# Local attention with V as the stationary operand in column tiles, and the first expert's gather placed inside the shared expert

## The chip, the cores and the metric

The kernel runs on one core of a Trainium2 chip. The metric is device time in microseconds (us), from launch to end; beside it stands the span of a profiled execution, from its first to its last instruction. PE is the matrix engine (TensorE), DVE the vector engine, ACT the scalar engine, POOL is GpSimd and SP the engine that issues most DMAs.

## The reference, cut to what matters

Three residual blocks on x (2 batches of 512 tokens, 512 wide), each on a layer-normalized x, all in float32: cross attention over 8192 context tokens per batch, local attention over a window of 7 tokens, and a mixture of 16 experts with a shared expert.

```python
# local attention, 16 heads of 32
q, k, v  = split_heads(x @ W_qkv.T + b_qkv)
k_lat    = k @ W_lat.T + b_lat          # per head, 32 x 32
v_lat    = v @ W_lat.T + b_lat
kw, vw   = k_lat[:, :, widx], v_lat[:, :, widx]    # 7 neighbours of each token, wrapping at the ends
attn     = softmax(einsum('bhsd,bhswd->bhsw', q, kw) / sqrt(32))
out      = einsum('bhsw,bhswd->bhsd', attn, vw) ; return out @ W_proj.T + b_proj

# experts: each takes the 128 tokens that score highest for it
topk_score, topk_ids = top_k(sigmoid(h @ gate_w.T).T, 128)
xin = h[topk_ids]
eo  = (silu(xin @ gw.T + gb) * (xin @ up_w.T + up_b)) @ down_w.T + down_b
out = zeros.at[topk_ids].add(eo * topk_score) + (silu(h @ sh_g.T) * (h @ sh_u.T)) @ sh_d.T
```

## The kernel before, in words

The stages follow each other: cross attention to about 2700 us of the profiled span, local attention to about 2915, the shared expert to 3089, the 16 experts to the end. They share one core, and PE's queue takes them in this order.

**Local attention** (lines 477 to 732). A group is one batch and four heads (128 channels); there are 8 groups. The 512 tokens of a group are cut into 5 blocks: four of 103 queries and one of 100. A block of `nq` queries meets `nk = nq + 6` keys, so its scores are a `nq` x `nk` matrix per head in which a band of 7 is kept (`band` adds -1e30 elsewhere). Per group, five `pieces` make the operands, each run beside one block of the group before: `project` of K (line 535), `latent_k` (line 562, then `extended`, which copies three wrapped columns to either end), `project` of Q, `project` of V, and `latent_v` (line 573), which makes V for each block with keys on partitions, 32 columns per head and a column of ones.

The loop over blocks (line 722) is pipelined by hand. Iteration k does, in this order:

- `softmaxed` of block k: four score matmuls, one per head, on 32 rows of the array each (`sw`, line 591); four DVE reduces that add the band and take the row maximum (line 599); the negated, scaled maximum (line 605); four ACT exps (line 607).
- one piece of the next group.
- `turned` of block k-1: four transposes of the exps on PE (`tpw`, line 618), one ACT copy to `pT`.
- `weighed` of block k-2: four matmuls with the turned exps stationary and V moving, 33 columns (`pow`, line 630). The column of ones gives the sum of the exps; DVE takes its reciprocal (line 635) and multiplies (line 637).
- `placed` of block k-3: a transpose back to channels on partitions (`tpo`, line 646), an ACT copy into `aT` (line 651), and after a batch's last block the output projection (`proj_residual`, line 106).
- what `beside` holds for this k: norms, inputs of the second batch, bias tables of the experts.

[...]

**Shared expert** (lines 773 to 806): for each batch 8 gate/up blocks (`pf`, line 780) and 4 output products of 8 matmuls each (`pso`, line 798). `select` is one of 16 rounds on DVE that find the 8 highest scores of each expert. After the stage the lists are turned by two small transposes (line 812) into `idx` and `scol`, whose columns address the gathers.

**Experts** (lines 875 to 893): `gather` reads 128 rows of the normalized tokens by an indirect DMA on POOL (line 822), `tokens` turns them on PE, `expert_in` streams weight tiles of 1 MB (`load_tile`, line 447, nine buffers in turn) and multiplies (line 839).

The framework that builds the instruction streams takes the code's order as priority, not as law: an instruction may be put ahead of an earlier one on its engine where it is ready. SP's timeline shows it: the first experts' weights are issued at 2874.7 us, long before the shared expert's outputs are stored.

Of the kernel before, what the change touches and what calls it, by code (L numbers as in the profile page):

```python
# [10 lines left out]
F32 = mybir.dt.float32  # L11
# [3 lines left out]
AF = mybir.ActivationFunctionType  # L15
ALU = mybir.AluOpType
# [27 lines left out]
def perceiver_kernel(  # L44
# [432 lines left out]
    with ExitStack() as es:  # L477
# [46 lines left out]
        def block(n):  # L524

            return n * BQ, min(BQ, S - n * BQ)
# [37 lines left out]

        def latent_v(i):

            vt = gp.tile([P, NBQ, 4, DK + 1], F32, name="vt")
            nc.gpsimd.memset(vt[:, :, :, DK : DK + 1], 1.0)
            for n in range(NBQ):
                q0, nq = block(n)  # L570
                nk = nq + W7 - 1
                pl = ps.tile([P, 4, DK], F32, tag="ps", name="plv")
                nc.tensor.matmul(
                    pl[0:nk].rearrange("p h d -> p (h d)"), lhsT=raw_t[i, 2][:, ds(q0, nk)],
                    rhs=wlat_bd, start=True, stop=True,
                )
                nc.vector.tensor_tensor(
                    vt[0:nk, n, :, 0:DK], pl[0:nk],
                    blat_b[0:nk].unsqueeze(1).to_broadcast([nk, 4, DK]), ALU.add,
                )  # L580
            v_t[i] = vt

        def softmaxed(i, n):

            q0, nq = block(n)
            nk = nq + W7 - 1
            ss = []
            for h in range(4):
                r = slice(h * DK, (h + 1) * DK)
                s = ps.tile([P, NK], F32, tag="ps", name="sw")  # L590
                nc.tensor.matmul(
                    s[0:nq, 0:nk], lhsT=q_t[i][r, ds(q0, nq)], rhs=k_t[i][r, ds(q0, nk)],
                    start=True, stop=True,
                )
                ss.append(s)
            sb = gp.tile([P, 4, NK], F32, name="sb")
            mx = gp.tile([P, 4], F32, name="mxw")
            for h in range(4):
                nc.vector.tensor_tensor_reduce(
                    out=sb[0:nq, h, 0:nk], in0=ss[h][0:nq, 0:nk], in1=band[0:nq, 0:nk],  # L600
                    scale=1.0, scalar=-3.0e38, op0=ALU.add, op1=ALU.max,
                    accum_out=mx[0:nq, h : h + 1],
                )
            nm = gp.tile([P, 4], F32, name="nm")
            nc.vector.tensor_scalar(nm[0:nq], mx[0:nq], -SCALE, None, ALU.mult)
            for h in range(4):
                nc.scalar.activation(
                    sb[0:nq, h, 0:nk], sb[0:nq, h, 0:nk], AF.Exp, bias=nm[0:nq, h : h + 1],
                    scale=SCALE,
                )  # L610
            p_t[i, n] = sb

        def turned(i, n):
# [9 lines left out]
            p_t[i, n] = t  # L623

        def weighed(i, n):
            q0, nq = block(n)
            nk = nq + W7 - 1
            po = ps.tile([P, 4, DK + 1], F32, tag="ps", name="pow")
            for h in range(4):
                nc.tensor.matmul(  # L630
                    po[0:nq, h, :], lhsT=p_t[i, n][0:nk, h, 0:nq], rhs=v_t[i][0:nk, n, h, :],
                    start=True, stop=True,
                )
            rl = gp.tile([P, 4, 1], F32, name="rlw")
            nc.vector.reciprocal(rl[0:nq], po[0:nq, :, DK : DK + 1])
            o = gp.tile([P, 4, DK], F32, name="ow")
            nc.vector.tensor_tensor(
                o[0:nq], po[0:nq, :, 0:DK], rl[0:nq].to_broadcast([nq, 4, DK]), ALU.mult
            )
            o_t[i, n] = o  # L640

        def placed(i, n):
            b, g = groups[i]
            q0, nq = block(n)
            tp = ps.tile([P, BQ], F32, tag="ps", name="tpo")
            nc.tensor.transpose(
                tp[:, 0:nq], o_t[i, n][0:nq].rearrange("p h d -> p (h d)"), ident[0:nq, 0:nq]
            )
            if g == 0 and n == 0:
                aT[b] = batch_tile("aT")  # L650
            nc.scalar.copy(aT[b][:, g, ds(q0, nq)], tp[:, 0:nq])
# [68 lines left out]
        for f in pieces:  # L720
            f(0)
        for k in range(len(items) + 3):
            if k < len(items):
                softmaxed(*items[k])
            i, n = divmod(k, NBQ)
            if i + 1 < len(groups):
                pieces[n](i + 1)
            for back, f in ((1, turned), (2, weighed), (3, placed)):
                if 0 <= k - back < len(items):
                    f(*items[k - back])  # L730
            for f in beside.get(k, ()):
                f()
# [23 lines left out]
    def select():  # L756
# [7 lines left out]
        if i < CAP // 8 - 1:  # L764
            nc.vector.match_replace(
                out=work[i % 2], in_to_replace=m8, in_values=cur, imm_value=-1.0
            )

    st = es1.enter_context(tc.tile_pool(name="s_tmp", bufs=2))
    sTp = es1.enter_context(tc.tile_pool(name="s_T", bufs=1))  # L770
    shd = [load_tile(sh_d[i]) for i in range(2)]
    norm(1, "f1")
    for b in range(B):
        sT = sTp.tile([P, SH // P, S], F32, tag="sT", name="sT")
        for f in range(SH // P):
            pair = []
            for wts in (shg, shu):
                pf = ps.tile([P, S], F32, tag="ps", name="pf")
                for c in range(DC):
                    nc.tensor.matmul(  # L780
                        pf, lhsT=wts[f // 4][:, c, ts(f % 4, P)], rhs=hT[b][:, c, :],
                        start=(c == 0), stop=(c == DC - 1),
                    )
                pair.append(pf)
            sg = st.tile([P, S], F32, name="sg")
            nc.scalar.activation(sg, pair[0], AF.Silu)
            nc.vector.tensor_tensor(sT[:, f, :], pair[1], sg, ALU.mult)
            if b == 0 and 1 <= f <= 4:
                forward_in(NT // B + f - 1, "f1")
            elif b == 0 and f == 5:  # L790
                gated(0)
                gated(1)
            elif b == 1 or f > 5:
                select()
        for j in range(4):
            po = ps.tile([P, D], F32, tag="ps", name="pso")
            for f in range(SH // P):
                nc.tensor.matmul(  # L798
                    po, lhsT=sT[:, f, ts(j, P)], rhs=shd[f // 4][:, f % 4, :],
                    start=(f == 0), stop=(f == SH // P - 1),  # L800
                )
            n = b * 4 + j
            nc.vector.tensor_tensor(x_sb[:, n, :], x_sb[:, n, :], po, ALU.add)
            nc.sync.dma_start(out=out[ts(n, P), :], in_=x_sb[:, n, :])
            select()
            select()

    top_f = sp.tile([E, CAP], F32, name="top_f")
    nc.vector.tensor_copy(top_f, top_i)
    for src, dst in ((top_f, idx), (top, scol)):  # L810
        pt = ps.tile([P, E], F32, tag="ps", name="pt")
        nc.tensor.transpose(pt, src, ident[0:E, 0:E])
        nc.vector.tensor_copy(dst, pt)
    es1.close()

    tmp = ctmp
    ep = ctx.enter_context(tc.tile_pool(name="e_tmp", bufs=2))

    def gather(e):

        xin = ep.tile([P, D], F32, name="xin")
        nc.gpsimd.indirect_dma_start(  # L822
            out=xin, out_offset=None, in_=h_dram,
            in_offset=bass.IndirectOffsetOnAxis(ap=idx[:, e : e + 1], axis=0),
        )
        return xin

    def expert_in(e, fq, xinT):

        pair = []  # L830
        for src, lo in ((gw, 0), (up, F)):
            wt = load_tile(src[e, fq])
            pf = ps.tile([P, 512], F32, tag="ps", name="pf")
            nc.tensor.matmul(
                pf, lhsT=pick[:, e, :], rhs=bias3[:, ds(lo + fq * 512, 512)],
                start=True, stop=False,
            )
            for c in range(DC):
                nc.tensor.matmul(  # L839
                    pf, lhsT=xinT[:, c, :], rhs=wt[:, c, :], start=False, stop=(c == DC - 1)  # L840
                )
            pair.append(pf)
# [22 lines left out]
            in_=y, in_offset=None, compute_op=ALU.add,  # L865
        )

    def tokens(xin):
        xinT = ep.tile([P, DC, CAP], F32, name="xinT")
        transposed(xinT, xin, ps)  # L870
        return xinT
# [69 lines left out]
```

## Time and profile before

| what | value |
|---|---|
| device time, median of 3 runs | 3846.05 us (3838.11 to 3847.68) |
| device time of the profiled execution | 3841.49 us |
| its span, first to last instruction | 3839.5 us |
| mean granted clock of PE | 0.993 |
| local attention, first latent V to the end of its last output projection | 2718.7 to 2915.1 us |
| shared expert, gate blocks and output products | 2915.1 to 3088.9 us |

In the profile's rows, `out<-in` names the tiles that an instruction writes and reads, then come partitions x elements. A matmul's form is given as rows * columns of the array that it occupies: `32*128` is a row tile, `128*32` a column tile. A float32 matmul appears as two records. A matmul's duration is latency; since matmuls overlap, what one takes from PE's time is the distance between the starts of neighbours. A row of a timeline begins with start and busy time in us and may end with the idle time before it and what released it.

### The profile page before, as it was taken

How to read it: one execution, taken by the hardware profiler on the slowest of the kernel's cores; microseconds unless marked ns; L12 is line 12 of the kernel's file. 1: busy time of each engine (PE TensorE's matmuls, PEld its weight loads, DVE VectorE, ACT ScalarE, POOL GpSimd, SP SyncE). 2: the span in 40 equal slices, each digit the busy share in tenths (PEclk: the TensorE clock that was granted, in tenths of full speed). 3: DMA queues.
4: the chain of work that ended last, by engine and by line, in shares of the span. 5: the costliest groups of instructions: out<-in, count | busy, mean ns of one | idle time of the engine just before them, and what ended most of it. 6: DMA issues, size and time to landing. Idle time of an engine off the chain costs nothing.

```text
span 3839.5 us, 99475 instructions
## 1 busy us (share of the span) xinstructions
PE 3773.4 (98%) x43100; PEld 1867.9 (49%) x43100; DVE 2284.6 (60%) x5444; ACT 1588.4 (41%) x2805; POOL 2069.1 (54%) x531
## 2 busy tenths in 40 slices
PE   8999999999999999999999999999999999999998
PEld 3345554554554554555555455444555444444444
DVE  6677777777777777777777777899743500000000
ACT  1125555555555555555555555676442001111110
POOL 0019998998998998999899899500100000000000
PEclk9999999999999999999999999999999999999999
DMA  5222212222223332222122222122201168888885
GB/s 188 87 73 71 69 60 70 71 71 71 71 68 103 125 125 92 70 71 71 57 71 71 71 71 70 60 86 63 75 31 36 58 229 286 285 287 287 288 285 172
DMA packets 143735, 438.07 MB, mean 114 GB/s; under 512 B 9408, under 2 KB 11728, under 8 KB 117856
## 3 DMA queue, kind: packets, MB, share of 16 engines
q1 hardware_dynamic: 137856, 419.33, 32.7%
q0 software_dynamic: 5200, 12.30, 1.3%
q8 instruction: 337, 5.52, 0.6%
q14 instruction: 102, 0.84, 0.1%
q10 hardware_dynamic: 240, 0.08, 0.0%
HBM read 423.21 MB, written 8.47 MB: 112 GB/s over the span
## 4 chain that ended last, share of the span: by engine, by line
PE 88%; DVE 2%; issue 1%; ACT 1%; DMA 0%; POOLq 0%; DVEq 0%; SPq 0%; ACTq 0%
PE av L353 13%; PE sx L295 12%; PE sc L331 12%; PE pv L255 11%; PE pf L839 11%; PE pk L239 10%; PE py L857 5%; PE pf L780 3%; PE sc L337 3%; PE pqkv L535 2%; PE po L106 1%; PE pso L798 1%; PE tp L98 1%; PE pow L630 1%; DVE junk L300 1%
## 5 line engine op out<-in xcount | busy, mean ns | idle before, releaser
L365 POOL TENSOR_TENSOR acc<-acc,pt 128x2048 f32<-128x2048 f32 x437 | 1991.2, 4557 | 452.0 <-ACT pt L344 451.2
L344 ACT ACTIVATE pt<-sc,mbias 128x512 f32<-128x512 f32 x2016 | 1218.3, 689 | 952.3 <-PE sc L337 950.9
L300 DVE CUSTOM_DVE_ANT_0 junk<-sx,mk 128x512 bf16<-128x512 f32 x1776 | 1228.1, 691 | 550.0 <-PE sx L295 352.7
L331 PE MATMUL sc<-qT,kt 32*128 32x512 f32 x4096 | 546.5, 594 | 0.0
L353 PE MATMUL av<-pt,vt 128*32 128x512 f32 x4032 | 540.6, 605 | 2.8 <-DVE mst L300 2.8
L255 PEld LDWEIGHTS pv<-wv_sb,ctx_t 128*32 128x32 f32 x16384 | 457.6, 110 | 155.0 <-DVE mst L300 101.4
L295 PE MATMUL sx<-kt,qT 32*128 32x512 f32 x3552 | 509.3, 640 | 0.9 <-DVE vt L260 0.9
L239 PE MATMUL pk<-ctx_t,wk_sb 128*32 128x256 f32 x8192 | 499.4, 385 | 2.1 <-DVE mst L300 2.1
L255 PE MATMUL pv<-wv_sb,ctx_t 128*32 128x128 f32 x16384 | 495.0, 273 | 1.3 <-DVE avs L361 1.3
L839 PE MATMUL pf<-wt,xinT 128*128 128x512 f32 x1024 | 460.9, 595 | 1.1
L239 PEld LDWEIGHTS pk<-ctx_t,wk_sb 128*32 128x32 f32 x8192 | 264.3, 111 | 298.1 <-DVE mst L300 104.7
L361 DVE TENSOR_TENSOR avs<-av,avs 128x512 f32<-128x512 f32 x504 | 345.6, 686 | 2.8 <-PE av L353 2.5
L331 PEld LDWEIGHTS sc<-qT,kt 32*128 32x128 f32 x4096 | 245.8, 185 | 200.8 <-issue 160.1
L846 DVE TENSOR_TENSOR eo<-pf,sg 128x512 f32<-128x512 f32 x64 | 44.3, 692 | 468.7 <-PE pf L839 468.7
L839 PEld LDWEIGHTS pf<-wt,xinT 128*128 128x128 f32 x1024 | 193.9, 191 | 222.0 <-issue 213.6
L822 POOL DMA_INDIRECT xin<-h_dram,idx x16 | 15.9, 992 | 444.2 <-PE tp L98 291.6
L863 POOL DMA_INDIRECT out_x<-y,idx x16 | 25.3, 1579 | 408.8 <-DVE y L862 408.8
L353 PEld LDWEIGHTS av<-pt,vt 128*32 128x32 f32 x4032 | 81.8, 108 | 325.8 <-DVE mst L300 281.0
L857 PE MATMUL py<-wt,eoT 128*128 128x512 f32 x512 | 222.3, 592 | 0.0
L844 ACT ACTIVATE sg<-pf 128x512 f32<-128x512 f32 x64 | 38.2, 597 | 422.1 <-PE pf L839 422.1
L337 PE MATMUL sc<-mT,neg 32*128 32x512 bf16 x2048 | 207.9, 374 | 0.0
L295 PEld LDWEIGHTS sx<-kt,qT 32*128 32x128 f32 x3552 | 140.0, 183 | 138.1 <-DVE mst L300 92.3
(161 smaller groups left out, 2504.6 us busy)
## 6 DMA issues: line engine op xcount, KB each, us to landing
ctx_t<-in_ctxT SPq DMA_DIRECT2D x160, 1024.0 KB, 6.0
wt<-in_gw SPq DMA_DIRECT2D x64, 1024.0 KB, 4.9
wt<-in_up SPq DMA_DIRECT2D x64, 1024.0 KB, 4.9
wt<-in_down SPq DMA_DIRECT2D x64, 1024.0 KB, 6.5
mk<-mrow SPq DMA_DIRECT2D x111, 256.0 KB, 3.5
ctx<-in_wqkv SPq DMA_DIRECT2D x3, 1024.0 KB, 5.3
mk<-mrow_h SPq DMA_DIRECT2D x17, 128.0 KB, 2.8
x_sb<-in_x SPq DMA_DIRECT2D x2, 1024.0 KB, 10.4
```

The costliest lines, as they stand in the source:

```text
L239: nc.tensor.matmul(pk[ts(h, DK), :], lhsT=wk_sb[:, c, ds(g * P + h * DK, DK)], rhs=ctx_t[slot, b][:, c, hs], start=(c == 0), stop=(c == DC ...
L255: nc.tensor.matmul(pv[ts(k, DK), i, :], lhsT=ctx_t[slot, b][:, c, ds((2 * half + i) * P + k * DK, DK)], rhs=wv_sb[:, c, ts(g, P)], start=( ...
L295: nc.tensor.matmul(sm, lhsT=qT[r, g, ds(b * S + c * P, P)], rhs=k_t[s][r, :], start=True, stop=True)
L300: nc.vector.tensor_tensor_reduce(out=junk, in0=ss[h], in1=mk_t[s], scale=1.0, scalar=-3.0e38, op0=ALU.add, op1=ALU.max, accum_out=mst[u][: ...
L331: nc.tensor.matmul(sc, lhsT=k_t[s][r, ts(ch, P)], rhs=qT[r, g, ts(b, S)], start=True, stop=False)
L337: nc.tensor.matmul(ss[h], lhsT=neg[r, :], rhs=m_t[u][r, :], start=False, stop=True)
L344: nc.scalar.activation(pt[:, h, :], ss[h], AF.Exp, bias=mbias[:, b, cc : cc + 1], scale=SCALE)
L353: nc.tensor.matmul(av[ts(h, DK), :], lhsT=v_t[s][:, ch, ts(h, DK)], rhs=pt_t[s, ch][:, h, :], start=True, stop=True,)
L361: nc.vector.tensor_tensor(avs[u], av, avs[u], ALU.add)
L365: eng.tensor_tensor(acc[u], acc[u], pt_t[s, ch], ALU.add)
L839: nc.tensor.matmul(pf, lhsT=xinT[:, c, :], rhs=wt[:, c, :], start=False, stop=(c == DC - 1))
L857: nc.tensor.matmul(py, lhsT=eoT[:, fq * 4 + c, :], rhs=wt[:, c, :], start=False, stop=(fq == FQ - 1 and c == 3),)
```

## The change

Local attention: `weighed` makes V the stationary operand, 32 columns per head in its own column tile, and lets the turned weights move, so the result has channels on partitions and goes straight to `aT`; `placed` and its transpose are gone, and the projection stays as `projected`. The division comes before the turn: the exps give their row sums by an accumulator output, and a new step `weights` takes the reciprocal and multiplies the whole block. Scores are made for blocks 0 and 1 together and for 2, 3 and 4 together, with one PSUM tile per head; `latent_v` makes four blocks in one PSUM tile and the last in another, without ones. Iteration k now does `weights` of k-1, `turned` of k-2, `weighed` and `projected` of k-3.

Shared expert: at batch 1's last gate block the lists are turned, expert 0's rows gathered and its first two weight tiles asked for; after the third output product of that batch its tokens are turned. The pools of this stage stay open through the experts.

```diff
         def latent_v(i):
-            vt = gp.tile([P, NBQ, 4, DK + 1], F32, name="vt")
-            nc.gpsimd.memset(vt[:, :, :, DK : DK + 1], 1.0)
-            for n in range(NBQ):
...
+            vt = gp.tile([P, NBQ, P], F32, name="vt")
+            for blocks in (range(NBQ - 1), (NBQ - 1,)):
+                pl = ps.tile([P, 4, P], F32, tag="ps", name="plv")
+                for n in blocks:
...
+        def softmaxed(i, blocks):
+            ss = [ps.tile([P, len(blocks), NK], F32, tag="ps", name="sw") for h in range(4)]
+            for m, n in enumerate(blocks):
...
+                for h in range(4):
+                    r = slice(h * DK, (h + 1) * DK)
+                    nc.tensor.matmul(
+                        ss[h][0:nq, m, 0:nk], lhsT=q_t[i][r, ds(q0, nq)],
+                        rhs=k_t[i][r, ds(q0, nk)], start=True, stop=True,
+                    )
+            for m, n in enumerate(blocks):
...
+                sb = gp.tile([P, 4, NK], F32, name="sb", bufs=5)
...
+                rl = gp.tile([P, 4, 1], F32, name="rlw", bufs=7)
+                for h in range(4):
+                    nc.scalar.activation(
+                        sb[0:nq, h, 0:nk], sb[0:nq, h, 0:nk], AF.Exp, bias=nm[0:nq, h : h + 1],
+                        scale=SCALE, accum_out=rl[0:nq, h, :],
+                    )
+                p_t[i, n] = sb, rl
+
+        def weights(i, n):
...
+            nc.vector.reciprocal(rl[0:nq], rl[0:nq])
+            nc.vector.tensor_tensor(
+                sb[0:nq, :, 0:nk], sb[0:nq, :, 0:nk], rl[0:nq].to_broadcast([nq, 4, nk]), ALU.mult
+            )
             p_t[i, n] = sb
...
         def weighed(i, n):
-            po = ps.tile([P, 4, DK + 1], F32, tag="ps", name="pow")
+            po = ps.tile([P, BQ], F32, tag="ps", name="pow")
             for h in range(4):
                 nc.tensor.matmul(
-                    po[0:nq, h, :], lhsT=p_t[i, n][0:nk, h, 0:nq], rhs=v_t[i][0:nk, n, h, :],
+                    po[ts(h, DK), 0:nq], lhsT=v_t[i][0:nk, n, ts(h, DK)],
+                    rhs=p_t[i, n][0:nk, h, 0:nq],
...
-            nc.vector.reciprocal(rl[0:nq], po[0:nq, :, DK : DK + 1])
...
-        def placed(i, n):
...
-            nc.scalar.copy(aT[b][:, g, ds(q0, nq)], tp[:, 0:nq])
+            nc.scalar.copy(aT[b][:, g, ds(q0, nq)], po[:, 0:nq])
...
         for k in range(len(items) + 3):
-            if k < len(items):
-                softmaxed(*items[k])
             i, n = divmod(k, NBQ)
+            if k < len(items) and n in (0, 2):
+                softmaxed(i, (0, 1) if n == 0 else (2, 3, 4))
...
-            for back, f in ((1, turned), (2, weighed), (3, placed)):
+            for back, f in ((1, weights), (2, turned), (3, weighed), (3, projected)):
...
+            elif b == 1 and f == SH // P - 1:
+                turned_lists()
+                xin = gather(0)
+                ahead = [load_tile(w[0, 0]) for w in (gw, up)]
             elif b == 1 or f > 5:
                 select()
...
-            select()
-            select()
+            if b == 0:
+                select()
+                select()
+            elif j == 2:
+                xinT = tokens(xin)
...
-    es1.close()
...
-            wt = load_tile(src[e, fq])
+            wt = ahead.pop(0) if ahead else load_tile(src[e, fq])
...
-    xinT, eoT, done = tokens(gather(0)), None, None
+    eoT, done = None, None
```

`turned_lists` holds the lines that stood after the stage: the cast of the indices (before at line 809), the two transposes and the two copies into `idx` and `scol`. `gather` and `tokens` are unchanged and only defined earlier.

More of the change, by code (lines that the diff above doesn't have):

```diff
@@ L565, in latent_v @@
         def latent_v(i):
-            vt = gp.tile([P, NBQ, 4, DK + 1], F32, name="vt")
-            nc.gpsimd.memset(vt[:, :, :, DK : DK + 1], 1.0)
-            for n in range(NBQ):
+            vt = gp.tile([P, NBQ, P], F32, name="vt")
+            for blocks in (range(NBQ - 1), (NBQ - 1,)):
+                pl = ps.tile([P, 4, P], F32, tag="ps", name="plv")
+                for n in blocks:
+                    q0, nk = block(n)[0], block(n)[1] + W7 - 1
+                    nc.tensor.matmul(
+                        pl[0:nk, n - blocks[0], :], lhsT=raw_t[i, 2][:, ds(q0, nk)],
+                        rhs=wlat_bd, start=True, stop=True,
+                    )
+                nb = len(blocks)
+                nc.vector.tensor_tensor(
+                    vt[0:nk, ds(blocks[0], nb), :].rearrange("p n (h d) -> p n h d", h=4),
+                    pl[0:nk, 0:nb, :].rearrange("p n (h d) -> p n h d", h=4),
+                    blat_b[0:nk].unsqueeze(1).unsqueeze(1).to_broadcast([nk, nb, 4, DK]), ALU.add,
+                )
@@ L570, in latent_v @@
+            v_t[i] = vt
+        def softmaxed(i, blocks):
+            ss = [ps.tile([P, len(blocks), NK], F32, tag="ps", name="sw") for h in range(4)]
+            for m, n in enumerate(blocks):
                 q0, nq = block(n)
                 nk = nq + W7 - 1
[L572 to L585, printed above, removed]
-            nk = nq + W7 - 1
[L587 to L610, printed above, removed]
@@ new lines, in softmaxed @@
+                for h in range(4):
+                    r = slice(h * DK, (h + 1) * DK)
+                    nc.tensor.matmul(
+                        ss[h][0:nq, m, 0:nk], lhsT=q_t[i][r, ds(q0, nq)],
+                        rhs=k_t[i][r, ds(q0, nk)], start=True, stop=True,
+                    )
+            for m, n in enumerate(blocks):
+                nq = block(n)[1]
+                nk = nq + W7 - 1
+                sb = gp.tile([P, 4, NK], F32, name="sb", bufs=5)
+                mx = gp.tile([P, 4], F32, name="mxw")
+                for h in range(4):
+                    nc.vector.tensor_tensor_reduce(
+                        out=sb[0:nq, h, 0:nk], in0=ss[h][0:nq, m, 0:nk], in1=band[0:nq, 0:nk],
+                        scale=1.0, scalar=-3.0e38, op0=ALU.add, op1=ALU.max,
+                        accum_out=mx[0:nq, h : h + 1],
+                    )
+                nm = gp.tile([P, 4], F32, name="nm")
+                nc.vector.tensor_scalar(nm[0:nq], mx[0:nq], -SCALE, None, ALU.mult)
+                rl = gp.tile([P, 4, 1], F32, name="rlw", bufs=7)
+                for h in range(4):
+                    nc.scalar.activation(
+                        sb[0:nq, h, 0:nk], sb[0:nq, h, 0:nk], AF.Exp, bias=nm[0:nq, h : h + 1],
+                        scale=SCALE, accum_out=rl[0:nq, h, :],
+                    )
+                p_t[i, n] = sb, rl
@@ L611, in softmaxed @@
+        def weights(i, n):
+            nq = block(n)[1]
+            nk = nq + W7 - 1
+            sb, rl = p_t[i, n]
+            nc.vector.reciprocal(rl[0:nq], rl[0:nq])
+            nc.vector.tensor_tensor(
+                sb[0:nq, :, 0:nk], sb[0:nq, :, 0:nk], rl[0:nq].to_broadcast([nq, 4, nk]), ALU.mult
+            )
             p_t[i, n] = sb
@@ L625, in weighed, with projected @@
         def weighed(i, n):
+            b, g = groups[i]
             q0, nq = block(n)
             nk = nq + W7 - 1
-            po = ps.tile([P, 4, DK + 1], F32, tag="ps", name="pow")
+            po = ps.tile([P, BQ], F32, tag="ps", name="pow")
             for h in range(4):
                 nc.tensor.matmul(
-                    po[0:nq, h, :], lhsT=p_t[i, n][0:nk, h, 0:nq], rhs=v_t[i][0:nk, n, h, :],
-                    start=True, stop=True,
-                )
-            rl = gp.tile([P, 4, 1], F32, name="rlw")
-            nc.vector.reciprocal(rl[0:nq], po[0:nq, :, DK : DK + 1])
[L636 to L640, printed above, removed]
-        def placed(i, n):
[L643 to L648, printed above, removed]
+                    po[ts(h, DK), 0:nq], lhsT=v_t[i][0:nk, n, ts(h, DK)],
+                    rhs=p_t[i, n][0:nk, h, 0:nq], start=True, stop=True,
+                )
             if g == 0 and n == 0:
                 aT[b] = batch_tile("aT")
-            nc.scalar.copy(aT[b][:, g, ds(q0, nq)], tp[:, 0:nq])
+            nc.scalar.copy(aT[b][:, g, ds(q0, nq)], po[:, 0:nq])
+        def projected(i, n):
+            b, g = groups[i]
             if g == G - 1 and n == NBQ - 1:
@@ L767, in select, with turned_lists, gather, tokens @@
             )
+    def turned_lists():
+        top_f = sp.tile([E, CAP], F32, name="top_f")
+        nc.vector.tensor_copy(top_f, top_i)
+        for src, dst in ((top_f, idx), (top, scol)):
+            pt = ps.tile([P, E], F32, tag="ps", name="pt")
+            nc.tensor.transpose(pt, src, ident[0:E, 0:E])
+            nc.vector.tensor_copy(dst, pt)
+    def gather(e):
+        xin = ep.tile([P, D], F32, name="xin")
+        nc.gpsimd.indirect_dma_start(
+            out=xin, out_offset=None, in_=h_dram,
+            in_offset=bass.IndirectOffsetOnAxis(ap=idx[:, e : e + 1], axis=0),
+        )
+        return xin
+    def tokens(xin):
+        xinT = ep.tile([P, DC, CAP], F32, name="xinT")
+        transposed(xinT, xin, ps)
+        return xinT
     st = es1.enter_context(tc.tile_pool(name="s_tmp", bufs=2))
     sTp = es1.enter_context(tc.tile_pool(name="s_T", bufs=1))
+    tmp = ctmp
+    ep = ctx.enter_context(tc.tile_pool(name="e_tmp", bufs=2))
     shd = [load_tile(sh_d[i]) for i in range(2)]
@@ L804, in perceiver_kernel @@
             nc.sync.dma_start(out=out[ts(n, P), :], in_=x_sb[:, n, :])
-            select()
-            select()
[L808 to L813, printed above, removed]
-    es1.close()
[L816 to L826, printed above, removed]
+            if b == 0:
[3 more added lines that the diff above has]
+                xinT = tokens(xin)
     def expert_in(e, fq, xinT):
@@ L866, in expert_out @@
         )
[L868 to L871, printed above, removed]
-    xinT, eoT, done = tokens(gather(0)), None, None
+    eoT, done = None, None
     for k in range(E * FQ + 1):
```

## The prediction

> **What bounds the kernel now.** I read the page's busy times and the chain that ended last first: TensorE (PE) is busy for 98% of the span and 88% of the chain is PE, so a saving counts only where it shortens PE's row of instructions or a stretch in which PE waits.
>
> ```profile
> PE 3773.4 (98%) x43100; PEld 1867.9 (49%) x43100; DVE 2284.6 (60%) x5444; ACT 1588.4 (41%) x2805; POOL 2069.1 (54%) x531
> PE 88%; DVE 2%; issue 1%; ACT 1%; DMA 0%; POOLq 0%; DVEq 0%; SPq 0%; ACTq 0%
> ```
>
> Then busy time by stretch (columns: stretch, length, then busy us and instruction count of PE, weight loads, DVE, ACT, POOL; granted clock, DMA share, GB/s): local attention's steady part (iterations 1 to 34 of the 40 blocks), its last blocks, and the seam before the experts.
>
> ```profile
> 2724.00:2884.20 160.20, 157.30 (x1005) 99.45 (x1004) 82.08 (x472) 84.41 (x237) 6.13 (x13) 1.00 0.08 27
> 2884.20:2900.00 15.80, 15.10 (x137) 12.43 (x137) 8.54 (x61) 11.36 (x38) 0.00 (x0) 0.87 0.04 14
> 3085.00:3106.00 21.00, 14.38 (x34) 6.36 (x33) 0.85 (x3) 1.18 (x2) 2.97 (x3) 0.84 0.56 183
> ```
>
> In the first PE is full and DVE and ACT are half idle; in the second ACT carries 11.4 of 15.8 us; in the third PE has a hole. Next, PE's own timeline of one iteration. "Busy" overlaps there, so I take start to start.
>
> ```profile
> 2776.05 0.45 PE L591 MATMUL sw<-ext,q_t 32*103 32x109 f32 x8
> 2776.43 3.70 PE L535 MATMUL pqkv<-xnT,ctx 128*128 128x512 f32 x8
> 2779.97 0.54 PE L618 MATMUL tpw<-ident,sb 103*109 103x103 f32 x4
> 2780.35 0.83 PE L630 MATMUL pow<-vt,pT 109*103 109x33 f32 x8
> 2781.01 0.29 PE L646 MATMUL tpo<-ident,ow 103*128 103x103 f32 x1
> 2781.23 0.44 PE L591 MATMUL sw<-ext,q_t 32*100 32x106 f32 x8
> ```
>
> So scores 0.38, projection 3.54, turning 0.38, weighing 0.66, turning the result back 0.22: 5.18 us. An f32 matmul is two records.
>
> **Change, part by part.** *Weighing* keeps 8 records, but V (32 columns) is stationary and 103 columns move, with four heads in four column tiles. This stage has no such matmul; the nearest rows are cross attention's, on the same 128*32 tiles (PE's timeline there):
>
> ```profile
> 1516.96 1.93 PE L255 MATMUL pv<-wv_sb,ctx_t 128*32 128x128 f32 x64
> 1518.82 1.14 PE L295 MATMUL sx<-kt,qT 32*128 32x512 f32 x8
> ```
>
> A 512-column record takes 0.43 us (eight from 3106.24 to 3109.68 in the seam's lines below), 0.84 ns a column. 64 records of 128 columns, one after another, would be 6.9 us; they took 1.86: four at a time (1.72) and 0.14 over. The scores, four row tiles, are 8 x 109 x 0.84 / 4 = 0.18 and took 0.38: about 0.20 is lost at entering and leaving the tiled mode. The new weighing by these rows: 8 x 103 x 0.84 / 4 = 0.17, plus 0.20 = 0.37, a saving of 0.29, for 40 blocks 11.6 us. The Trainium skill has a rule against this step ("TensorEngine Tiling (Array Packing)", Key Properties): a change of tiling mode, not of tile alone, drains the array, and the change adds two such switches a block. It gives no price; "TensorE: Matmul & The Clock Gate" (Part 2) gives some 128 cycles for the last column, 53 ns at its 2.4 GHz, by which (an estimate) the weighing is 0.17 + 0.11 = 0.28 and the saving 15. I take the row, 11.6; ends: 18 if switches are free, -1 if the heads don't overlap (8 x 103 x 0.84 = 0.69).
>
> *Turning back* goes: 40 x 0.22 = 8.8 us. *Scores in 16 bursts* in place of 40: same matmuls, 24 switches into and out of row tiles fewer, 24 x 0.20 = 4.8. Together 25.2 us of PE, 0.63 a block. Only the 35 blocks before the last group lie where PE sets the pace: 22.
>
> *ACT* gets an accumulator output on 160 exps. No ACT row of this kernel has one. Rows that bound it (group view):
>
> ```profile
> L607 ACT ACTIVATE sb<-sb,nm 103x109 f32<-103x109 f32 x128 | 38.9, 375 | 45.5 <-DVE nm L605 45.4
> L599 DVE DVE_READ_ACCUMULATOR2_ANT mxw<- 103x1 f32 x128 | 10.6, 83 | 0.0
> L651 ACT COPY aT<-tpo 128x103 f32<-128x103 f32 x32 | 7.8, 242 | 3.9 <-PE tpo L646 3.0
> L637 DVE TENSOR_TENSOR ow<-pow,rlw 103x128 f32<-103x128 f32 x32 | 9.3, 290 | 0.6
> L111 DVE TENSOR_TENSOR x_sb<-x_sb,prt 128x512 f32<-128x512 f32 x9 | 6.2, 692 | 0.3
> ```
>
> DVE's separate read is 83 ns. If ACT's read is an instruction of its own, it costs about the fixed part of a small ACT one: the copy's 242 ns less 103 x 0.84 = 0.16 us. "ScalarE: Activation LUTs" (What ACT_TABLE_LOAD costs) says 186 ns fixed and 93 overlapped back to back, so 0.09 to 0.19, which would make the sum below 84.4 + 12 to 26; I take 0.16, with ends 0.08 and 0.30 (a 128x4 ACTIVATE, L84, 298 ns). In the steady part ACT then has 84.4 + 34 x 4 x 0.16 = 106 us in 160.2 - 34 x 0.63 = 139: 76%, hidden behind PE; the cover is gone at 0.40 an exp. In the last group nothing hides it: 20 x 0.16 = +3.2, less about 1.2 for the reciprocal, product and turn that ended the old chain (the last weighing's start at 2897.7 to the last aT copy at 2900.3 held them): +2.
>
> *DVE* loses the product of 103x128 (0.29) and gets one of 103x436: between the two rows above 1.05 ns a column, 0.61. The reciprocal stays (0.18). +0.32 x 34 = 11 on 82: 93 of 139, hidden. V's five additions become two, POOL's memset goes: off the path. The twelve reduces of a three-block burst (0.19 each, 2.3 us) stand ahead of the older block's reciprocal and product; the transposes that wait for these come an iteration later, behind a projection of 3.5 us.
>
> *New waits.* The latent products (pl, plv) follow a projection whose ACT copy (0.69, for V two DVE copies more) must end. Before, turning, weighing, turning back and scores (1.64 us) stood between; now turning and weighing (0.75), since those two iterations have no scores. In the order of the code 0.3 to 0.5 us is missing, 14 times: 4 to 7 us. The streams aren't held to that order (in the last blocks tpw and pow alternate, and SP issued the experts' first weights at 2874.7), so later scores can fill part: +3, ends 0 and 7. Stage: -22 + 2 + 3 = -17 us.
>
> *First gather.* The seam, PE's timeline:
>
> ```profile
> 3088.98 0.21 PE L812 MATMUL pt<-ident,top 16*128 16x16 f32 x1
> 3095.80 1.09 PE L98 MATMUL tp<-ident,xin 128*128 128x128 f32 x4 [6.62 <-DMA xin<-h_dram,idx]
> 3096.69 1.06 PE L834 MATMUL pf<-bias,pick 96*128 96x512 bf16 x2
> 3106.03 0.38 PE L834 MATMUL pf<-bias,pick 96*128 96x512 bf16 x1
> 3106.24 3.60 PE L839 MATMUL pf<-wt,xinT 128*128 128x512 f32 x8
> 3109.68 0.38 PE L834 MATMUL pf<-bias,pick 96*128 96x512 bf16 x1
> ```
>
> From the last shared matmul (3088.89) to the third bias row is 17.1 us: a 6.6 us hole, after which PE runs at a granted clock of 0.50, then 0.68, so that two weight tiles take 9.3 us in place of 2 x 3.65. Without it: two list transposes 0.2, four token transposes 0.45, 7.3: 7.95. Saving 9.2. What each moved instruction meets: DVE's cast of the indices already ran at 3028.9, 32 us before the last gate block ends (3061.3), so PE doesn't wait for it; two DVE copies of 0.17; the gather finds POOL idle for 152 us, takes 1.0 to issue and 3.3 to 5.0 to land, under three output products of 6.87 each. If that cover failed, the 9.2 would come back. The two weight loads pass four output stores on SP, but SP had issued them at 2874.7 and 2879.9 anyway: 0. The experts then start 9 us earlier on nine tiles already asked for; PE waits for no weights there now.
>
> **Sum.** -17 - 9 = -26 us against the profiled execution's own span, 3839.5, and time, 3841.5: 3815. That run is 4.5 below the median shown (3846.05), inside its 3838 to 3848; I take 3816.
>
> **Rivals.** (1) *The tail fills too*: the shared expert's gate matmuls are ready by 2892.5 and go into the last group's gaps. Then its PE saving (5 x 0.63 = 3) counts, the latents cost 0 and the half clock around 2896 to 2902 (some 2 us) goes: about 3806. For: SP's loads run ahead. Against: before, these matmuls came only after the output projection. (2) *ACT becomes the bound*: reads of 0.35 to 0.45 in bursts of 12 exps; the stage gains about 7, with the gather 16: 3829. Against: 76% load. (3) *The heads don't overlap*: with two records of a head back to back in a tile, the weighing stays 0.66: 35 x 0.29 = 10 less, 3826. For: only 103 columns. Against: the scores, just as short, overlap. (4) *Slower*: the accumulator read at 0.7 us an exp. ACT then needs 84.4 + 136 x 0.7 = 180 us in the steady part against 160 now (+20), the last group +13, the gather -9: 3865. It decides from 0.6 on, where +6, +11 and -9 pass 0.3%; no ACT row with so little data is above 0.3. (5) *The gather's wait goes over to the first weights*, 3825: against, seven tiles were asked for by then.
>
> **How the numbers follow.** Chances: forecast 0.58 (its own range 3805 to 3827), (1) 0.14, (2) 0.12, (3) 0.10, (4) 0.04, (5) 0.02. 0.3% is 11.5 us, about what a measurement of this kernel tells from no change. The range 3800 to 3832 leaves out (4), a third of (2) and the outer part of (1), with some spread of runs. Above 3834.5 lie (4) and the last of (2): faster 0.91, same 0.05, slower 0.04.
>
> **What would show it.** In the iteration with Q's projection PE should need 3.5 + 0.38 + 0.37 + about 0.75 for three blocks' scores; tpo is gone; pow is 109*32 and start to start some 0.37 us. ACT in the stage stays under 85%, with accumulator reads near 0.16. The seam has no PE hole, with a clock of 1.0. Wrong, if pow keeps 0.66, if PE waits for sb or ext more than 7 us in total, if the reads cost over 0.4, or if the hole at the seam stays under another name.

## The result, and the profile after

The changed kernel takes 3814.39 us (median of 5 runs, 3808.77 to 3821.03), the kernel before in the same rounds 3838.11 (3834.79 to 3847.68). The ratio is 0.9932, 95% interval 0.9918 to 0.9946: faster by 0.7%. The profiled execution has a span of 3811.6 us, 27.9 less than the 3839.5 of before.

Where the 27.9 us lie is read from the starts of instructions that both kernels have. The table holds the distances between them.

| stretch | before | after | difference |
|---|---|---|---|
| start to local attention's first projection (code unchanged) | 2705.23 | 2699.58 | -5.65 |
| from there to the first block's scores | 14.77 | 14.78 | 0 |
| loop: first block's scores to the last group's first scores | 164.21 | 148.96 | -15.25 |
| last group: from there to the first gate matmul (output projection in it) | 30.86 | 32.94 | +2.08 |
| shared expert and seam: first gate matmul to the third bias row | 190.96 | 181.89 | -9.07 |
| experts: from there to the end | 733.47 | 733.45 | 0 |

From the first projection to the third bias row is *the changed stretch*: 400.80 us before, 378.57 after, -22.2. All experiments below are read by it too, since it holds all that they edit.

The first row varies by itself, with PE's granted clock at the start of the program. The first 300 us, before and after:

```profile
0.00:300.00 300.00, 277.26 (x2930) 119.72 (x2934) 202.13 (x253) 52.62 (x96) 30.86 (x17) 0.94 0.34 112
0.00:300.00 300.00, 275.25 (x2998) 120.00 (x3002) 205.69 (x263) 55.55 (x101) 36.27 (x18) 0.97 0.36 116
```

To three digits the clock is 0.943 and 0.966; 0.023 of 300 us is 6.9 us of clock, enough for the 5.65. The twelve profiles of this study keep that order: at a clock of 0.943 there, local attention starts at 2705.2 to 2705.8 us, at 0.949 to 0.960 at 2700.4 to 2703.8, at 0.966 at 2699.2 to 2699.6.

How far can one profile be trusted in the changed stretch? Two pairs of profiles have the same local attention: before and the gather alone, the change and the attention alone (the last two come below). Within a pair, the loop and the part of the last group ahead of the output projection agree to 0.02 us. The output projection does not: it takes 15.06 and 16.06 us with the old attention, 16.54 and 15.26 with the new, as more or less of a spell of low clock falls on it. In these four projections (before, gather alone, after, attention alone) the clock was:

```profile
2900.00:2915.10 15.10, 15.10 (x34) 6.62 (x34) 6.79 (x12) 1.52 (x2) 0.00 (x0) 0.91 0.00 1
2894.10:2910.20 16.10, 16.10 (x34) 7.05 (x34) 6.78 (x12) 1.53 (x2) 0.00 (x0) 0.86 0.00 1
2879.70:2896.30 16.60, 16.60 (x37) 7.27 (x34) 6.79 (x12) 1.53 (x2) 0.00 (x0) 0.83 0.00 0
2881.00:2896.30 15.30, 15.30 (x37) 6.79 (x34) 6.78 (x12) 1.52 (x2) 0.00 (x0) 0.90 0.00 0
```

So a difference of up to some 1.5 us between two profiles may be this alone. Ahead of the projection the last group took 15.80 us before and 16.40 after; of its +2.08 only these 0.6 recur in both pairs.

The page's busy times of after:

```profile
PE 3741.4 (98%) x43060; PEld 1835.4 (48%) x43060; DVE 2293.9 (60%) x5420; ACT 1601.8 (42%) x2965; POOL 2069.0 (54%) x523
```

PE lost 32 us of 3773 and stays the bound. Busy time by stretch, for after's loop, its last group up to the output projection, and the seam (columns as before):

```profile
2714.40:2863.30 148.90, 141.54 (x977) 77.79 (x976) 93.96 (x468) 94.88 (x381) 5.45 (x8) 1.00 0.08 26
2863.30:2879.70 16.40, 11.52 (x144) 7.73 (x140) 8.11 (x56) 13.36 (x58) 0.00 (x0) 0.75 0.12 49
3057.00:3078.10 21.10, 21.10 (x54) 9.42 (x53) 1.94 (x3) 1.18 (x2) 0.95 (x1) 1.00 0.54 186
```

The same loop before, from its first scores on:

```profile
2720.00:2884.20 164.20, 161.30 (x1021) 101.16 (x1020) 83.51 (x483) 85.63 (x241) 6.13 (x13) 1.00 0.08 27
```

In the loop PE's busy time fell by 19.8 us, while its idle time rose from 2.9 to 7.4. In the last group PE is busy for 11.5 of 16.4 us, at a mean clock of 0.75. The seam is now full, at a clock of 1.00. PE's timeline of two iterations of after, with K's projection and then latent K:

```profile
2773.18 0.64 PE L592 MATMUL sw<-ext,q_t 32*103 32x109 f32 x16
2773.75 3.70 PE L535 MATMUL pqkv<-xnT,ctx 128*128 128x512 f32 x8
2777.29 0.54 PE L633 MATMUL tpw<-ident,sb 103*109 103x103 f32 x4
2777.76 0.39 PE L647 MATMUL pow<-pT,vt 109*32 109x103 f32 x8
2778.69 1.13 PE L562 MATMUL pl<-raw,wlat_bd 128*128 128x512 f32 x2 [0.55 <-ACT raw L545]
2779.65 0.51 PE L633 MATMUL tpw<-ident,sb 100*106 100x100 f32 x4
2780.09 0.39 PE L647 MATMUL pow<-pT,vt 109*32 109x103 f32 x8
2780.40 0.82 PE L592 MATMUL sw<-ext,q_t 32*103 32x109 f32 x24
2781.16 3.70 PE L535 MATMUL pqkv<-xnT,ctx 128*128 128x512 f32 x8
```

Scores of two blocks take 0.57, of three 0.76, where single ones took 0.38 each. The weighing takes 0.31 (2780.09 to 2780.40). The turning in front of it has grown from 0.38 to 0.47, though its four transposes are the same. The transpose back is gone.

The kernel before had such a step of 0.09 in another place: its transpose back took 0.21 or 0.22 where scores in row tiles followed, but 0.12 where transposes on the full array did. One of the latter, in before:

```profile
2759.02 0.28 PE L646 MATMUL tpo<-ident,ow 103*128 103x103 f32 x1
2759.14 0.60 PE L98 MATMUL tp<-ident,xn 128*128 128x128 f32 x4
```

Back in after, between the weighing's end (2777.76 + 0.31) and the latent product PE stands still for 0.62 us. The groups of instructions that the forecast's sum rested on:

```profile
L611 ACT ACTIVATE sb<-sb,nm 103x109 f32<-103x109 f32 x128 | 47.5, 374 | 18.9 <-DVE nm L608 18.9
...
L611 ACT ACTIVATION_READ_ACCUMULATOR sb<-sb,nm 103x1 f32 x128 | 24.0, 187 | 0.0
...
L623 DVE TENSOR_TENSOR sb<-sb,rlw 103x436 f32<-103x436 f32 x32 | 19.5, 611 | 0.7
```

The accumulator read is an instruction of its own, 187 ns by its row. DVE's new product takes the 0.61 us that was forecast. Now the seam, PE's timeline:

```profile
3042.70 0.21 PE L780 MATMUL pt<-ident,top 16*128 16x16 f32 x1
3042.84 20.87 PE L833 MATMUL pso<-wt,sT 128*128 128x512 f32 x48
3063.54 0.60 PE L98 MATMUL tp<-ident,xin 128*128 128x128 f32 x4
3063.98 7.03 PE L833 MATMUL pso<-wt,sT 128*128 128x512 f32 x16
3070.85 0.38 PE L852 MATMUL pf<-bias,pick 96*128 96x512 bf16 x1
```

No hole: the lists' transposes and the tokens' stand among the output products.

### The profile page after: what moved, and what is told of

Same layout as the page of the kernel before. It is cut to its first block, busy times and chain, and to the rows that moved or that the text cites. A ratio compares the mean times of both kernels' runs of the same rounds, so it can differ in the third digit from the quotient of the medians.

```text
span 3811.6 us, 99469 instructions
## 1 busy us (share of the span) xinstructions
PE 3741.4 (98%) x43060; PEld 1835.4 (48%) x43060; DVE 2293.9 (60%) x5420; ACT 1601.8 (42%) x2965; POOL 2069.0 (54%) x523
## 4 chain that ended last, share of the span: by engine, by line
PE 87%; DVE 2%; ACT 2%; issue 1%; DMA 0%; POOLq 0%; DVEq 0%; ACTq 0%
PE av L353 13%; PE sx L295 12%; PE sc L331 12%; PE pv L255 11%; PE pf L857 11%; PE pk L239 10%; PE py L875 5%; PE pf L810 3%; PE sc L337 3%; PE po L106 2%; PE pqkv L535 2%; PE pso L833 1%; PE tp L98 1%; DVE junk L300 1%; ACT sb L611 1%
```

## The experiments

Theory A, as I held it after this comparison: two separate savings, in local attention's loop and at the seam; the 5.65 us in front are no part of the change; what the loop lost against the forecast is PE waiting for the latent products. The rivals are named in the expectations. Ratios are to the kernel before, timed in the same session; lengths of stretches come from one profile of each kernel.

### Each half alone

```diff
 # e1_attention_only, against the change: the seam as before
-            elif b == 1 and f == SH // P - 1:
-                turned_lists()
-                xin = gather(0)
...
+    xinT, eoT, done = tokens(gather(0)), None, None
```

> The change's local attention alone, the first gather back behind the shared expert. Theory A (two separate savings: 13 us in local attention's stage, from the first Q/K/V projection to the first gate matmul, and 9 at the seam; the 5.6 us by which cross attention ended earlier in the profile after is no part of the change): the stage takes 197 us against 210 before, the seam keeps its hole of 6.6 us, in all about -13 us. Theory B (cross attention's 5.6 us come with the new local attention, by where its tiles lie): -19, and cross attention ends at 2699 to 2700 us again.

```diff
 # e2_gather_only, against the kernel before: the seam of the change
+            elif b == 1 and f == SH // P - 1:
+                turned_lists()
+                xin = gather(0)
+                ahead = [load_tile(w[0, 0]) for w in (gw, up)]
...
+            elif j == 2:
+                xinT = tokens(xin)
```

> The kernel before with the first gather, lists and tokens inside the shared expert. Theory A: -9 us, all of it between the first gate matmul and the third bias row (191 us before, 182 expected), the experts behind it as long as before (733.5). Theory B would have cross attention end at 2705 as before if it hangs on local attention, near 2700 if it hangs on the pools that stay open. Rival C (the hole only goes over to the weights once PE runs on): a PE wait for wt of some us in the first expert, and less than -4.

Measured: attention alone 0.9952 (0.9938 to 0.9965), its changed stretch 386.33 us (-14.5), with shared expert and seam at 190.95 as before. The gather alone 0.9968 (0.9957 to 0.9979), 392.73 us (-8.1): -9.07 from the first gate matmul to the third bias row, and +1.0 in local attention, in the output projection. The experts took 733.36 and 733.24 us. The halves add: -22.5 against -22.2 together. Rival C falls. Theory B falls too: local attention's first projection began at 2700.9 with the new attention and at 2699.3 with the old, and between 2699.2 and 2705.8 in all twelve profiles. These two alone would fit a theory B in which either half pulls the start forward, but three later kernels hold both halves and start at 2705.5 to 2705.8. The start goes with the clock of the first 300 us, as shown above.

### Scores of one block at a time

```diff
-            if k < len(items) and n in (0, 2):
-                softmaxed(i, (0, 1) if n == 0 else (2, 3, 4))
+            if k < len(items):
+                softmaxed(i, (n,))
```

> The changed kernel with the scores of one block at a time, one burst in each iteration, as before the change. By the trace a group's bursts of 2 and 3 take 0.57 and 0.76 of PE, five single ones 1.9: +0.57 a group, +4.6 in all. But a burst then stands again in front of the latent products, where PE now waits 0.62 (K) and 0.37 us (V) a group. Theory A: the waits fall to under 2 us in the loop (from about 7) and the two nearly cancel: local attention's loop changes by -2 to +2 us against the changed kernel. Rival D (the waits for the latents come from ACT's exps with their accumulator reads, not from the lack of scores): the waits stay and the loop is 4 to 5 us longer.

Measured: 0.9927 (0.9912 to 0.9943); the changed stretch 380.87 us, 2.3 more than the change. PE's waits for `pl` in the loop fell from 4.6 to 0.4 us, and PE's idle time in the loop fell from 7.4 to 3.7. The sum of the waits for `plv` stayed (2.8 and 2.7), but not what it is made of: in the change one of 1.6 in the first group and four of 0.3, here one of 2.4 in the first group and one of 0.3. The loop itself is 3.7 us longer, outside theory A's range, for a reason that neither theory had. PE's timeline, first group:

```profile
2738.43 1.53 PE L572 MATMUL plv<-wlat_bd,ext 128*109 128x128 f32 x10 [2.41 <-DVE ext L552]
...
2742.79 5.42 PE L535 MATMUL pqkv<-xnT,ctx 128*128 128x512 f32 x8
```

One wait of 2.4 us is followed by a spell at a granted clock of 0.72 and 0.86 (two stretches of 8 us), in which the next projection takes 5.26 us from start to start, not 3.54. Against the same instructions elsewhere in this trace the spell costs 3.2 us. Without it PE's busy time is 145.8, 4.3 above the change's 141.5, and the idle time 3.7 below: the bursts save on PE what the forecast said, and give nearly all of it back as a wait for K's copy. That part of theory A holds. The first group's wait for V is not cured by scores: there ACT's copy of V starts 1.9 us after its projection's end (2736.81 and 2734.96).

### Exps without their row sums

```diff
+                nc.gpsimd.memset(rl, 1.0)
...
-                        scale=SCALE, accum_out=rl[0:nq, h, :],
+                        scale=SCALE,
```

> The changed kernel without the accumulator output of the exps: the row sums are left out (a tile of ones is divided by), the rest stays. By the trace an exp's step falls from 0.37 to 0.28 us, ACT's work by 160 x 0.09 = 15 us. Theory A (ACT is hidden in the loop and sets only the last group's pace): the last group is 1.5 to 2 us shorter, the loop within 1 us, in all -2. Rival D (the reads hold up the copies that the latent products wait for): the waits of pl and plv, 7 us in all, go too and the loop is 4 to 7 us shorter.

Measured: 0.9916 (0.9900 to 0.9931); the changed stretch 370.66 us, 7.9 less than the change: the loop 4.5 less, the last group 3.4 (2.6 ahead of the output projection, 0.8 in it). Theory A is wrong here and rival D is right in good part: PE's idle time in the loop falls from 7.4 to 3.1 us. ACT's timeline of the change, the end of the burst of eight exps and the copy behind it (accumulator reads left out), and of this kernel:

```profile
2777.23 0.37 ACT L611 ACTIVATE sb<-sb,nm 103x109 f32<-103x109 f32 x1
...
2777.60 0.37 ACT L611 ACTIVATE sb<-sb,nm 103x109 f32<-103x109 f32 x1
...
2777.97 0.67 ACT L545 ACTIVATE raw<-pqkv,bqkv_c 128x512 f32<-128x512 f32 x1
```

```profile
2778.36 2.32 ACT L612 ACTIVATE sb<-sb,nm 103x109 f32<-103x109 f32 x8 [1.32 <-DVE nm L608]
2780.85 0.69 ACT L545 ACTIVATE raw<-pqkv,bqkv_c 128x512 f32<-128x512 f32 x1 [0.17 <-PE pqkv L535]
```

Without sums the exps end at 2780.68 and the copy of K starts when its projection is done. With them an exp's step is 0.37 in place of 0.28, eight take 2.97, and the copy starts the moment the last one ends. By the distance from the next transposes' start (2780.65 without sums, 2777.29 with them) to the copy, 0.20 and 0.68, with the sums the copy is 0.48 us late, and by about as much or more in each of the loop's seven groups. PE's pause in front of `pl` falls from 0.62 to 0.16. The waits for `pl` sum to 1.6 us where the change has 4.6, those for `plv` to 1.5 where it has 2.8: the one of 1.6 in the first group is down to 0.3, the four of 0.3 are unchanged.

### Scores in front of the latent products

```diff
-            if k < len(items) and n in (0, 2):
-                softmaxed(i, (0, 1) if n == 0 else (2, 3, 4))
+            if k == 0:
+                softmaxed(0, (0, 1))
+            if k < len(items) and n == 1:
+                softmaxed(i, (2, 3, 4))
+            elif n == NBQ - 1 and i + 1 < len(groups):
+                softmaxed(i + 1, (0, 1))
```

> The changed kernel with its two bursts of scores moved in front of the latent products: blocks 2, 3 and 4 in the iteration of latent K, the next group's blocks 0 and 1 in that of latent V; the buffers of exps go from 5 to 6, those of V from 3 to 2. Theory E (what the loop lost against the forecast is PE waiting for pl and plv: 0.46 us of pl's wait a group is K's copy behind exps with row sums on ACT, the rest is the missing cover of the scores): both go, PE's idle time in the loop falls from 7.4 us to about 2, the loop is 5 to 6 us shorter, in all about -6 against the changed kernel (some 0.15%). Rival F (the exps of the larger burst now delay other copies, and the wait appears at the transposes or at the next projection): PE idles as long as before under another name, no gain.

Measured: 0.9936 (0.9918 to 0.9953); the changed stretch 378.13 us, 0.4 less than the change: rival F. The latents' waits in the loop shrank from 4.6 and 2.8 to 0.6 and 0.4 us, and a new wait came, of the weighing for `pT`: 8.5 us in the loop, 12.0 with the last group. From the first scores to the output projection PE stands still for 13.2 us, where it did for 12.2 in the change. PE's and ACT's timelines show one of these:

```profile
2790.79 0.54 PE L633 MATMUL tpw<-ident,sb 103*109 103x103 f32 x4
2792.32 0.38 PE L647 MATMUL pow<-pT,vt 106*32 106x100 f32 x8 [0.99 <-ACT pT L637]
```

```profile
2790.86 0.37 ACT L611 ACTIVATE sb<-sb,nm 100x106 f32<-100x106 f32 x1
...
2791.22 0.66 ACT L551 ACTIVATE ext<-pl,blat_c 128x512 f32<-128x512 f32 x1
2791.79 0.47 ACT L637 COPY pT<-tpw 106x400 f32<-106x400 f32 x1
```

Twelve exps in a row hold ACT for 4.4 us (2786.79 to 2791.23). Behind them stand K's copy into `ext` and then the copy of `pT`, for which PE waits now. In both places tried, the burst delays a copy that PE needs.

### Gate blocks in the last group, and both edits

```diff
+        at(38, gate_matmuls, 0, 0)
+        at(40, gate_matmuls, 0, 1)
```

`gate_matmuls(b, f)` makes the 8 gate and up matmuls of one block.

> The changed kernel with the first two gate/up blocks of the shared expert (16 matmuls, 13.7 us of PE) emitted beside iterations 38 and 40, inside the last group, where PE idles and its clock falls. Theory A (the last group is paced by ACT and PE has 6 to 8 us free there): the stretch from the last group's first scores to the output projection's end takes some of the 13.7 in, and the clock stays at 1.0; -6 against the changed kernel, ends -9 and -3. Rival G (the 3.4 us lumps of gate matmuls stand in front of transposes that ACT waits for): the last group grows by as much as is filled, 0.

> Both edits on the changed kernel: scores in front of the latent products, gate blocks in the last group. Theory A with E: the gains add, about -11 against the changed kernel (3803 where that takes 3814), 0.95% below the kernel before. With rival F or G one half of it is missing.

Measured: 0.9941 (0.9926 to 0.9956) and the changed stretch 380.21 us, 1.6 more than the change; both edits together 0.9939 (0.9923 to 0.9956), 379.87 us. That is rival G's case; with F, neither half of the last run gained. PE's timeline of the first of the two kernels:

```profile
2872.59 1.03 PE L633 MATMUL tpw<-ident,sb 103*109 103x103 f32 x4 [0.89 <-DVE sb L623]
2875.04 0.57 PE L647 MATMUL pow<-pT,vt 109*32 109x103 f32 x8 [1.43 <-ACT pT L637]
2875.66 9.21 PE L714 MATMUL pf<-hT,wt 128*128 128x512 f32 x16
```

The gaps are still there and the gate matmuls come after them, in a lump of 9 us, mostly at the low clock, in front of the next transposes. The last copy of `hT`, which every gate matmul reads, ended only at 2875.6 here, just before the lump; in the change's profile it stood behind the exps and ended at 2874.8.

### Row sums on DVE; gate matmuls small and early; both

```diff
 # e8_sums_on_dve (e10 too)
-                        scale=SCALE, accum_out=rl[0:nq, h, :],
+                        scale=SCALE,
...
+            nc.vector.tensor_reduce(rl[0:nq, :, 0], sb[0:nq, :, 0:nk], AX.X, ALU.add)
             nc.vector.reciprocal(rl[0:nq], rl[0:nq])
 # e9_gates_in_gaps (e10 too)
-        at(29, norm, 0, "f0")
-        for i, k in enumerate((31, 33, 35, 37)):
+        at(24, norm, 0, "f0")
+        for i, k in enumerate((26, 28, 30, 32)):
             at(k, forward_in, i, "f0")
+        at(37, gate_some, 2)
+        at(38, gate_some, 2)
+        at(39, gate_some, 2)
+        at(40, gate_some, 2)
+        at(41, gate_some, 4)
+        at(42, gate_some, 4)
```

`gate_some(n)` makes the next n of the first two blocks' 16 gate and up matmuls.

> The changed kernel with the row sums taken by a DVE reduce over the block, in the step of the division, and no accumulator output on the exps. Theory H (the accumulator reads cost time through the order of ACT's queue, where bursts of exps stand in front of the copies that PE waits for, though ACT is only 64% busy in the loop; without sums the stage was 7.9 us shorter): the stage takes 188 to 191 us against 196.7, -6 to -8 in all. Rival I (DVE, 63% busy in the loop, gets 40 x 0.5 = 20 us more, and the wait goes over to its bursts): 194 to 197, no gain.

> The changed kernel with the shared expert's tokens of batch 0 made five iterations earlier (in the run with the gate blocks in the last group their last copy stood behind exps on ACT until 2874, so the gates could only come as lumps after the gaps) and the first two gate blocks emitted by two or four matmuls beside iterations 37 to 42. Theory A (PE has some 5 us of gaps there and runs at half clock from 2872 to 2884): from the first projection to the third bias row 378.6 us becomes 372 to 375. Rival G (the matmuls in ACT's way cost as much as they fill): 378 to 380.

> Both: sums on DVE, early tokens and split gate blocks. If H and A hold the gains add: from the first projection to the third bias row 378.6 becomes 365 to 369, some 10 us below the changed kernel, near 0.9% below the kernel before. If ACT alone held the last group, the gate matmuls have less to fill and it is 369 to 372.

Measured:

| kernel | device time | ratio to before (95%) | changed stretch | against the change |
|---|---|---|---|---|
| e8, sums on DVE | 3812.50 | 0.9919 (0.9905 to 0.9933) | 373.55 | -5.0 |
| e9, gates in gaps | 3811.42 | 0.9922 (0.9909 to 0.9935) | 374.21 | -4.4 |
| e10, both | 3807.90 | 0.9907 (0.9894 to 0.9921) | 370.17 | -8.4 |

With the sums on DVE the loop falls by 2.8 us and the last group by 2.2, of which 0.6 lie ahead of the output projection and 1.6 in it, where equal kernels differ by 1.3; the stage is 191.7, between the two ranges and nearer to theory H's. ACT's busy time in the loop goes from 94.9 to 82.6 and DVE's from 94.0 to 109.2. PE's wait for `pl` in the loop falls from 4.6 to 1.2 us, that for `plv` stays at 2.6, and one new wait comes, 0.6, for `pT`; in the last group one of 3.1 us appears, for the sums and their reciprocal on DVE. So the same sums cost less on an engine that was as busy: in the loop they stand in a queue behind which PE waits for less.

With early tokens and small lots the gate matmuls do fill gaps. PE's timeline of e9 in the last group:

```profile
2867.68 1.03 PE L633 MATMUL tpw<-ident,sb 103*109 103x103 f32 x4 [1.35 <-DVE sb L623]
2868.72 0.56 PE L647 MATMUL pow<-pT,vt 106*32 106x100 f32 x8
2869.21 5.44 PE L728 MATMUL pf<-hT,wt 128*128 128x512 f32 x6
2874.49 0.54 PE L633 MATMUL tpw<-ident,sb 103*109 103x103 f32 x4
```

From the last group's first scores to the third bias row e9 takes 210.1 us against the change's 214.8; its output projection runs at full speed, 14.0 us. Early tokens and small lots were not tried apart. In e10 the gains come to 8.4 us where their sum is 9.4. Its 370.2 us lie in the expectation's second case, but only 1.2 us from the first, too little for one profile of each to decide. By device time e10 is the fastest kernel of the study; none of these kernels was timed beside the change itself, and the intervals of e8, e9 and e10 touch its 0.9918 to 0.9946, so what each gains over the change rests on the stretches.

## Why the prediction was right, and where it was off

The forecast was 3816 us by a gain of 26 on the profiled execution; the time came in at 3814, and the changed stretch gave 22.2. That 22 and not 26 hit the time so closely is in part luck: the kernel before ran at 3838 in these rounds, not at the 3846 shown.

- **The seam** (-9.2): it gave 9.07, alone or with the rest. The hole, the low clock behind it and the lists that are ready long before were as worked out, and PE waits for no weights in the experts' first tiles.
- **PE's own work in the loop** (0.63 a block, -22): 0.59 a block by the starts, -19.8 in busy time. The scores' bursts gave 0.57 a group, as forecast. The weighing fell to 0.31, not 0.37, but turning in front of it takes 0.47, not 0.38; together 0.78 against 0.75. The 0.09 looks like the entry into the tiled mode, since the kernel before has it ahead of its row tiles. The Trainium skill's rule in "TensorEngine Tiling (Array Packing)" (Key Properties), that a switch of mode drains the array, fits this: a switch costs here about what the row said, not the 53 ns of my estimate from the other page. That the cost is a drain, no run here shows. (One end of that sum was wrong: with free switches 40 weighings would save 40 x 0.49 = 20, not 18.)
- **The accumulator read** (0.16 us an exp): 0.09 by the step of the exps. "ScalarE: Activation LUTs" (What ACT_TABLE_LOAD costs) of the Trainium skill gives 186 ns fixed and 93 overlapped back to back for an ACTIVATE: the read's row has 187, and the step grew by 0.093. Here the lower end of what I took from the page was right and my estimate from the copy too high.
- **"ACT hidden behind PE in the loop"**: this is the step that failed. It was argued from ACT's share, 76% forecast, 64% measured. The share hides that the exps now come in bursts of 8 and 12, and that K's copy stands behind one of them. Leaving the sums out gained 4.5 us in the loop; the forecast had 0 for them there.
- **New waits** (+3, by missing scores): PE's idle time rose by 4.5, from 2.9 to 7.4, and the cause was only half named. With the sums left out it is 3.1, though no scores stand in front of the latent products there either; with single scores and the sums it is 3.7. So most of the wait needs both, copies held up by the exps and no scores to cover them. The 0.3 to 0.5 us that the forecast found missing in each of 14 places is, without the sums, 0.09 in four groups for K and 0.29 in four for V. The forecast's sign of being wrong, more than 7 us of waits for `sb` or `ext`, was not met (5.2), but it did not name `raw`, K's copy, where the largest wait came (4.6).
- **The last group** (+2): +0.6 ahead of the output projection. The sums cost 2.6 there (16.40 us with them, 13.77 without; forecast 3.2), and the old chain's end gave 2.0 (15.80 to 13.77; forecast 1.2). The other 1.5 of the +2.08 lie in the output projection, which differs by 1.0 and 1.3 between equal kernels; with the attention alone it is 0.2 longer than before. That the size came out as forecast is luck.

Of the rivals, ACT as the bound is refuted by its load, but its mechanism, exps in bursts, works below that bound. The filled tail didn't come by itself; the run in which it came had earlier tokens and small lots.

## What to carry to other kernels

A row of the nearest kind of tile, read from start to start, gives the cost of a new matmul form well, if the switch into its tiling mode is looked for in the instruction ahead of it. An in-order engine at two thirds of its time can still set the pace: ask what stands behind its longest burst, and who waits for that; moving the burst may only change whom it delays, as here, and moving part of its work to another queue can help even if that engine is as busy. Work meant to fill gaps has to have its inputs before the gaps, and be cut to their size.

## What the runs showed of the hardware that was not expected

PE's clock fell in the last group of the change without a long pause: no PE gap there is over 1.6 us, yet the granted clock was 0.94, 0.50 and 0.50 in three stretches of 4 us:

```profile
2868.00:2872.00 4.00, 1.85 (x17) 1.32 (x18) 3.25 (x27) 4.00 (x21) 0.00 (x0) 0.94 0.00 0
2872.00:2876.00 4.00, 2.58 (x24) 1.73 (x23) 1.70 (x5) 3.45 (x16) 0.00 (x0) 0.50 0.00 0
2876.00:2880.00 4.00, 3.87 (x41) 2.28 (x34) 0.00 (x0) 2.16 (x7) 0.00 (x0) 0.50 0.01 4
```

It came back only behind the output projection's first 512-column matmuls. The gaps don't explain it, though: in the kernel before, the clock fell in the last group too, after 11 us in which no PE gap was over 0.2 us. Stretches of before:

```profile
2892.00:2896.00 4.00, 3.96 (x34) 2.86 (x33) 2.15 (x16) 3.65 (x13) 0.00 (x0) 0.97 0.00 0
2896.00:2900.00 4.00, 3.51 (x20) 3.22 (x20) 0.95 (x4) 1.09 (x5) 0.00 (x0) 0.50 0.00 0
```

So a row that shows PE almost always busy does not keep the clock. In all twelve profiles it fell in the last group, where the loop's 512-column projections no longer stand between the short matmuls; in the loop it fell in two (scores of one block, scores in front of the latent products). Which property of the work the clock answers to was not tried. In the run with single scores the spell in the loop followed one wait of 2.4 us; in the change's loop none followed a wait of 1.6.
